# Splitting a router's dispatch into single-instruction steps, and moving its sums, in a two-layer transformer kernel

## The chip, the cores and the metric

The kernel runs on one core of one Trainium2 chip. The metric is the device time of one execution in microseconds (us), less is better. A core has five engines that run their own instruction streams: TensorE (PE, matrix products), VectorE (DVE), ScalarE (ACT), GpSimd (POOL), and SyncE (SP), which here only issues DMAs. PE writes its results to the memory PSUM, whose parts are called banks; the other engines read them from there. Everything else on the chip lies in SBUF.

## The reference

Two transformer layers on x of 4 batch elements x 1024 tokens x 256 features, all in float32. Layer 0 is attention with 16 heads, normalised queries and keys and rotary positions, followed by a gated feed-forward. Layer 1 is causal attention with 8 heads, followed by a mixture of experts. After each of the four parts the input is added and a layer norm is taken. The change concerns the mixture of experts, whose core is:

```python
xn = _rmsnorm(x_flat, norm_weight, EPS)
probs = softmax(xn @ router_weight.T + router_bias)
gate_vals, expert_idx = top_k(probs, 2)
pos = sum(cumsum(one_hot) * one_hot) - 1      # place in the expert's queue
keep = pos < CAP                              # CAP = 512
dispatch = zeros((16, CAP, 256)).at[expert, slot].add(xn[tok] * keep)
# expert 0: zeros; 1: copy of the row; 2, 3: constant vectors; 4 to 15: MLPs
w = gate_vals * keep
out = sum(expert_out[expert, slot] * w) / (sum(w) or 1)
x = layernorm(x + out)
```

Queues run over all tokens in order, so the positions of one batch element depend on the counts of those before it, and an expert's rows are complete only when the last element has been dispatched.

## The kernel before

**Stages.** For each element b there are four pieces of work: the first attention (`first_units(b)`, 64 units), the first feed-forward, the second attention (`second_units(b)`, 29 units) and the router with its dispatch. The program works on them in a weave: it goes through the units of one attention and sets pieces of other work behind each unit. Within this part nothing is rescheduled (`manual_schedule`): on every engine instructions stand in the order in which the code emits them. `later(n, fn)` puts a function off by n units; `tick()` at the start of a unit runs those due.

For elements 0 and 1, `weave` takes one step of `dispatch(b)` per unit of `first_units(b + 2)`, from unit `side_at` on. For element 2 and for the first half of element 3 ("3a") there is a hand-written table `plan`: `plan[u]` lists what follows unit u of `second_units(3)`. The second half of element 3 ("3b") follows after the last unit, then the twelve MLP experts one after another, about 29 us each, then the last layer norm.

**second_units.** A unit can hold: scores of one block of keys (`sc`, L964: four heads, each once with the keys and once with the maxima), values and denominators of the block before it (`av`, `dn`, L1001), and a maxima unit (`mx`, L914), whose four results DVE reduces (L924 on the diagonal, L928 elsewhere). Units 20 to 28 have no maxima. All these PE results and other "big" pieces share six PSUM banks in turn; a bank is free again when DVE or ACT has read it. ACT takes the exponential (L975), POOL zeroes the upper triangle on the diagonal (`affine_select`, L978), DVE takes reciprocals of the denominators (L1019), POOL multiplies with them (L1021). Behind the units stand the output projection (`ppa`, L572) with its residual addition and statistics on DVE (L539 to L542), the roots on POOL (L105), the normalisation on DVE (L109), the transposition of x for the router (`ptxn`, L622) and the logits (`pl`, L693).

**dispatch.** Its steps are: `choose(0)` and `choose(1)` (largest logits and their experts, L742 to L753), `queue` (counts, L758 to L761), `positions` (two matmuls into `pos`, L767 and L768, and their copy L769), `slots` (L774 to L785: the slot numbers `si`), `weights` (L789 to L805: weights `w`, the row's tail `meta`, the shares `we`), `stage` (L815, L818: two rows xn and their tails in `st`), `send` (two indirect DMAs of one row of 128 tokens to `disp_d`, issued by POOL, L824) and `base` (three multiply-adds on DVE that add the copy's and the constant vectors' shares to x, L836 and L840, then a store of x to `acc_d` on SP, L843). For elements 0 and 1 one step was `send` and `base` of one row of tokens. For elements 2 and 3 the `base` functions, "sums", were emitted behind the ordered part, so that the scheduler set them in between:

```python
        for step in steps3[10:] + more:
            step()
        ordered.close()
        for step in sums2 + sums3 + sums:
            step()
```

**Behind it.** `load_rows(0)` loads the first expert's rows in four parts (L1408, waiting for every send), `transpose_to` turns them (`ptd`, L98) and copies them to `dmT` (L99), `ph` (L1439) and `py` (L1455) are the expert's two products, and an indirect DMA adds its results to `acc_d` (L1459), for expert 0 only after the stores of all sums. The pools for `dm`, `dmT` and others take over the memory of the pools before them, x among it.

Of the kernel before, what the change touches and what calls it, by code (L numbers as in the profile page):

```python
# [19 lines left out]
P = 128  # L20
# [15 lines left out]
def postln_layers_kernel(ctx: ExitStack, tc: tile.TileContext, a: dict, out: bass.AP):  # L36
# [53 lines left out]
    spacer = const.tile([P, 1], F32, name="spacer")  # L90


    def transpose_to(dst, src, pool, name):

        n = dst.shape[1]
        pt = pool.tile([P, 512], F32, tag="m", name=name)
        for i in range(n):
            nc.tensor.transpose(pt[:, i * P : (i + 1) * P], src(i), ident)  # L98
        nc.any.tensor_copy(dst, pt[:, : n * P].rearrange("p (n q) -> p n q", n=n))  # L99
# [11 lines left out]
    with ExitStack() as main:  # L111
# [598 lines left out]
        def dispatch(b, big, part=None):  # L710
# [20 lines left out]
            def choose(k):  # L731
# [3 lines left out]
                if k == 0:  # L735
# [3 lines left out]
                    for key in ("g", "ei", "pk", "keep", "w", "step"):  # L739
                        v[key] = act.tile([P, 2, n], F32, tag=f"v_{key}", bufs=1, name=f"{key}_{name}")  # L740
# [21 lines left out]

            def positions():

                flat = v["both"].rearrange("p t e -> p (t e)")
                pos = bank(f"pos_{name}", big)[:, : n * E]
                nc.tensor.matmul(pos, before, flat, start=True, stop=False)  # L767
                nc.tensor.matmul(pos, ones, v["cum"].rearrange("p t e -> p (t e)"), start=False, stop=True)  # L768
                nc.vector.tensor_copy(flat, pos)  # L769

            def slots():
                pk, keep, w, ei, step = [v[key] for key in ("pk", "keep", "w", "ei", "step")]
# [3 lines left out]
                none = none_f[:, :, rows]  # L776
                nc.vector.tensor_scalar(keep, pk, float(CAP), None, ALU.is_lt)
                nc.vector.tensor_tensor(w, w, keep, ALU.mult)
                nc.vector.tensor_scalar(step, ei, -float(EM), None, ALU.is_ge)
                nc.vector.tensor_tensor(keep, keep, step, ALU.mult)  # L780
                nc.vector.scalar_tensor_tensor(pk, ei, float(CAP), pk, ALU.mult, ALU.add)
                nc.vector.scalar_tensor_tensor(pk, pk, float(NSLOT), none, ALU.add, ALU.subtract)
# [4 lines left out]
            def weights():  # L787
                gs, gz, w = small("gs"), small("gz"), v["w"]
# [5 lines left out]
                v["meta"] = meta = act.tile([P, n, 4], F32, tag="v_meta", bufs=1, name=f"meta_{name}")  # L794
                nc.vector.tensor_copy(meta[:, :, 0], v["ei"][:, 0])
                nc.vector.tensor_tensor(meta[:, :, 1], w[:, 0], w[:, 1], ALU.subtract)
                nc.vector.tensor_copy(meta[:, :, 2], w[:, 1])
                nc.vector.tensor_copy(meta[:, :, 3].bitcast(I32), tok_i[:, rows])
                v["we"] = we = act.tile([P, n, 3], F32, tag="v_we", bufs=3, name=f"we_{name}")
                wo = v["oh", 1][:, :, 1:4]  # L800
                for k, t in enumerate((we, wo)):
                    nc.vector.tensor_tensor(
                        t, v["oh", k][:, :, 1:4], w[:, k].unsqueeze(2).to_broadcast([P, n, 3]), ALU.mult
# [9 lines left out]
            def stage(i):  # L813
                v["st", i] = st = late_tile(b, [P, 2, ROW], F32, "xn", 12, f"row_{name}_{i}")
                nc.vector.tensor_copy(st[:, :, C:ROW], v["meta"][:, 2 * i : 2 * i + 2, :])  # L815
                for t in (2 * i, 2 * i + 1):
                    r, u = st[:, t % 2, :], first + t
                    nc.vector.scalar_tensor_tensor(r[:, 0:C], xs[b, u], rrs[b][:, u : u + 1], nw, ALU.mult, ALU.mult)  # L818
# [15 lines left out]
            def base(t):  # L834
                x, u = xs[b, first + t], first + t
                nc.vector.scalar_tensor_tensor(  # L836
                    x, v["st", t // 2][:, t % 2, 0:C], v["we"][:, t, 0:1], x, ALU.mult, ALU.add
                )
                for k in range(2):
                    nc.vector.scalar_tensor_tensor(  # L840
                        x, v["cv"][:, k], v["we"][:, t, 1 + k : 2 + k], x, ALU.mult, ALU.add
                    )
                based.append(nc.sync.dma_start(acc_rows[:, b * TB + u, :], x).ins)  # L843
                if b + 2 < B:
                    load_x(b + 2, u)

            def both_steps(t):
                send(t)
                base(t)

            out = [lambda: choose(0), lambda: choose(1), queue, positions, slots, weights]
            if b < B - 2:
                for i in range(n // 2):
                    out += [lambda i=i: stage(i), lambda i=i: both_steps(2 * i), lambda i=i: both_steps(2 * i + 1)]
                return out
            out += [lambda i=i: stage(i) for i in range(n // 2)] + [lambda t=t: send(t) for t in range(n)]
            return out, [lambda t=t: base(t) for t in range(n)]

        sent, based = [], []

# [437 lines left out]
        for b in (1, 2):  # L1298
# [16 lines left out]
                30,  # L1315
# [25 lines left out]
        steps2, sums2 = dispatch(2, True)  # L1341
        steps3, sums3 = dispatch(3, True, 0)
# [15 lines left out]
        for u, step in enumerate(steps2[:5]):  # L1358
            plan[12 + u].append(step)
        plan[17] += steps2[5:8]  # L1360
        plan[18] += steps2[8:10]
        for u, step in enumerate(steps2[10:]):
            plan[18 + u].append(step)
        for u, p in ((16, out3[0]), (17, out3[1]), (18, tu[0]), (19, lo[0]), (19, tu[1]), (20, lo[1])):
            plan[u].append(lambda p=p: p(True))
        for u, step in enumerate(steps3[:5]):
            plan[21 + u].append(step)
        plan[26] += steps3[5:8]
        for u in range(2):
            plan[27 + u].append(steps3[8 + u])  # L1370
# [17 lines left out]
        more, sums = dispatch(3, True, 1)  # L1388
        for step in steps3[10:] + more:
# [188 lines left out]
```

## Time and profile before

| | |
|---|---|
| median of 3 runs | 2486.8 us (2482.63 to 2492.3) |
| profiled execution, its own time | 2493.76 us |
| its span, first to last instruction | 2492.0 us |
| mean granted TensorE clock | 0.949 |
| second_units(3), first maxima to last values | 1887 to 2060 us |
| element 3's last projection to the first expert | 2062 to 2107.6 us |
| twelve experts | 2107.6 to 2458 us |

All durations below are of the one profiled execution. A line of the timeline has the start and the time of a group in us, the engine, the line of the code, the operation, what it writes and reads, how many instructions it has, and in brackets how long the engine stood idle ahead of it and who released it. A line of the windows has start and end, length, busy time of the engine with its instructions, granted clock, share of the DMA engines and GB/s. DVE operations of a dozen to a hundred elements take 0.16 to 0.29 us, one of 256 elements 0.4 to 0.5.

### The profile page before, as it was taken

The page shows a single profiled execution, that of the slowest core. Times are in us where ns is not written, and L with a number is a line of the kernel's source. Part 1 is how long each engine was busy: PE and PEld are TensorE (multiplying, and loading weights), DVE is VectorE, ACT ScalarE, POOL GpSimd, SP SyncE. Part 2 cuts the span into 40 slices and gives each one's busy share as a digit, 9 for nine tenths or more (in the row PEclk, how much of TensorE's full clock was granted, in tenths as well). Part 3 has the DMA queues.
Part 4 walks back from the last instruction along what each step waited for, and adds up shares of the span by engine and source line. Part 5 has one row for each costly group of instructions (what it writes and reads, how often), then busy time and mean ns, then how long its engine had stood idle before and what let it go on. Part 6 is the DMA issues. An engine that isn't in the chain of part 4 may idle for free.

```text
span 2492.0 us, 36155 instructions
## 1 busy us (share of the span) xinstructions
PE 2331.3 (94%) x14004; PEld 1156.8 (46%) x14004; DVE 1384.9 (56%) x3227; ACT 1020.2 (41%) x2037; POOL 743.9 (30%) x1101
## 2 busy tenths in 40 slices
PE   7999998999999999999999999999999974999994
PEld 4433333444444443444444434445556432666662
DVE  6666664766656556686574767806645674111113
ACT  2465554554552445545433464462232231111112
POOL 5234536125204132363051420301112154212223
PEclk9999998999998999999899999998999686999997
DMA  3124212000000000011000000102000012444434
GB/s 96 56 95 143 70 44 70 1 27 1 1 27 1 1 1 1 23 46 33 32 1 1 1 1 1 62 7 99 1 1 1 1 52 69 102 107 114 105 88 146
DMA packets 78124, 107.77 MB, mean 43 GB/s; under 512 B 8832, under 2 KB 67200, under 8 KB 76288
## 3 DMA queue, kind: packets, MB, share of 16 engines
q1 hardware_dynamic: 48592, 73.34, 9.0%
q0 software_dynamic: 9984, 14.82, 3.1%
q10 hardware_dynamic: 19376, 17.30, 2.3%
q8 instruction: 110, 1.80, 0.3%
q14 instruction: 62, 0.51, 0.1%
HBM read 66.54 MB, written 38.90 MB: 42 GB/s over the span
## 4 chain that ended last, share of the span: by engine, by line
PE 86%; DVE 7%; DMA 3%; POOL 2%; issue 1%; ACT 1%; SPq 0%; DVEq 0%; ACTq 0%; POOLq 0%
PE sc L474 19%; PE av L492 10%; PE ph L1439 7%; PE gu L638 7%; PE py L1455 7%; PE sc L964 5%; PE mx L914 4%; PE mx L450 4%; PE p L883 4%; PE dn L654 4%; PE av L1001 3%; PE dn L1001 2%; PE ppa L572 2%; DVE masked L924 2%; PE qk L303 2%; PE pt L441 1%
## 5 line engine op out<-in xcount | busy, mean ns | idle before, releaser
L453 DVE TENSOR_REDUCE part<-mx 128x1 f32<-128x512 f32 x1024 | 655.6, 683 | 338.0 <-PE mx L450 331.7
L483 ACT ACTIVATE pe<-sc 128x512 f32<-128x512 f32 x1024 | 554.2, 596 | 401.5 <-PE mx L450 349.2
L450 PE MATMUL mx<-kT,qT 32*128 32x512 f32 x2048 | 631.4, 646 | 2.1 <-DVE part L453 1.9
L474 PE MATMUL sc<-qT,kT 32*128 32x512 f32 x2048 | 606.4, 639 | 0.0
L474 PEld LDWEIGHTS sc<-qT,kT 32*128 32x128 f32 x2048 | 176.4, 183 | 220.3 <-issue 178.4
L492 PE MATMUL av<-pe,va 128*32 128x512 f32 x2048 | 273.9, 607 | 0.0
L975 ACT ACTIVATE pe<-sc 128x512 f32<-128x512 f32 (+3 forms) x384 | 157.2, 496 | 216.8 <-PE sc L964 216.5
L450 PEld LDWEIGHTS mx<-kT,qT 32*128 32x128 f32 x2048 | 188.2, 185 | 40.0 <-DVE part L453 18.6
L924 DVE CUSTOM_DVE_ANT_0 masked<-mx,mask_w 128x128 bf16<-128x128 f32 (+3 forms) x256 | 125.2, 489 | 122.0 <-PE mx L914 89.8
L1439 PE MATMUL ph<-dmT,f 128*128 128x512 f32 x384 | 170.5, 602 | 4.3 <-DVE dmT L99 3.5
L1447 ACT ACTIVATE hTm<-ph,b 128x512 f32<-128x512 f32 x96 | 60.8, 684 | 261.5 <-PE ph L1439 261.5
L1455 PE MATMUL py<-f,hTm 128*128 128x256 f32 x768 | 167.7, 379 | 0.0
L978 POOL TENSOR_SCALAR_AFFINE_SELECT pe<-pe 128x256 f32<-128x256 f32 x128 | 54.4, 434 | 370.7 <-ACT pe L975 369.2
L1459 POOL DMA_INDIRECT acc_d<-yo,dm x48 | 74.7, 1556 | 285.3 <-DVE yo L1457 233.9
L1455 PEld LDWEIGHTS py<-f,hTm 128*128 128x128 f32 x768 | 145.9, 190 | 25.0 <-issue 5.7
L914 PE MATMUL mx<-kT,qT 32*128 32x512 f32 (+3 forms) x768 | 142.4, 593 | 3.8 <-DVE x L539 3.2
L368 POOL TENSOR_TENSOR ss<-ss,neg_half 128x16 f32<-128x16 f32 x48 | 139.2, 2908 | 0.5
L964 PE MATMUL sc<-qT,kT 32*128 32x512 f32 (+3 forms) x768 | 133.6, 591 | 4.0 <-DVE part L924 2.5
L1456 DVE TENSOR_TENSOR yo<-py,b 128x256 f32<-128x256 f32 x48 | 20.4, 425 | 208.1 <-PE py L1455 208.1
L492 PEld LDWEIGHTS av<-pe,va 128*32 128x32 f32 x2048 | 40.5, 108 | 194.1 <-issue 188.7
L1439 PEld LDWEIGHTS ph<-dmT,f 128*128 128x128 f32 x384 | 72.9, 192 | 95.0 <-issue 86.9
L638 PE MATMUL gu<-xTf,wg 128*128 128x256 f32 x384 | 107.2, 401 | 0.3 <-ACT pe L975 0.3
(346 smaller groups left out, 2976.9 us busy)
## 6 DMA issues: line engine op xcount, KB each, us to landing
f<-in_fc SPq DMA_DIRECT2D x14, 1024.0 KB, 4.9
f<-in_fc ACTq DMA_DIRECT2D x10, 1024.0 KB, 5.9
disp_d<-empty ACTq DMA_DIRECT2D x12, 520.0 KB, 3.4
xink<-in_xT SPq DMA_DIRECT2D x24, 256.0 KB, 3.2
qk_d<-xs SPq DMA_DIRECT2D x6, 1024.0 KB, 3.9
xr<-qk_d SPq DMA_DIRECT2D x6, 1024.0 KB, 6.1
dm<-disp_d SPq DMA_DIRECT2D x11, 520.0 KB, 3.6
x<-in_x SPq DMA_DIRECT2D x32, 128.0 KB, 2.9
```

The costliest lines, as they stand in the source:

```text
L450: nc.tensor.matmul(sc, self.qT[r, t * P : (t + 1) * P], self.kT[r, u * 512 : (u + 1) * 512], start=True, stop=True)
L453: return lambda: nc.vector.tensor_reduce(self.part[:, t, u, h : h + 1], sc, AX.X, ALU.max, negate=True)
L474: nc.tensor.matmul(sc, self.m.kT[r, kt * P : (kt + 1) * P], self.m.qT[r, qb * 512 : (qb + 1) * 512], start=True, stop=True)
L483: nc.scalar.activation(self.pes[i, h // 2][:, h % 2, :], sc, AF.Exp)
L492: nc.tensor.matmul(self.av[32 * h : 32 * h + 32, :], va0[:, kt, 4 * self.g + h, :], self.pes[i, h // 2][:, h % 2, :], start=kt == 0, stop= ...
L638: nc.tensor.matmul(ps[:, i * 256 : (i + 1) * 256], w[:, c, f * P : (f + 1) * P], xT[j][:, c, :], start=c == 0, stop=c == 1,)
L914: nc.tensor.matmul(scs[h][:, :n], qT[r, t * P : (t + 1) * P], kT[r, u * 512 : u * 512 + n], start=True, stop=True,)
L924: nc.vector.tensor_tensor_reduce(masked[:, :n], scs[h][:, :n], mask_w[:, 512 - n :], -1.0, -NEG, ALU.add, ALU.min, part)
L964: nc.tensor.matmul(scs[h][:, off:], ones_h[r, :] if w else kT[r, kt * P : (kt + 1) * P], (self.m.nmT if w else qT)[r, q], start=w == 0, st ...
L975: nc.scalar.activation(pe[:, j, off:], scs[2 * hp + j][:, off:], AF.Exp)
L1439: nc.tensor.matmul(ph[:, i * CAP : (i + 1) * CAP], f1[:, c, (f + i) * P : (f + i + 1) * P], dmT[:, c, :], start=c == 0, stop=c == 1,)
L1455: nc.tensor.matmul(py[:, :C], hT[:, f, c * P : (c + 1) * P], f2[:, f, :], start=f == 0, stop=f == FF1 // P - 1)
```

## The change

The steps of the dispatch are cut smaller and set anew. What needs no positions (`prepare`, `row`) is a step of its own ahead of what does; `positions` is split from its copy `places`; `shares` is split from `weights`; a row's tail (`ends`) is split from the row. For elements 0 and 1 every multiply-add of a sum is a step of its own, and the steps begin at unit 26. In the plan element 2's sums follow units 20 to 27, three multiply-adds each, and the turn and logits of element 3's x come one unit later. Element 3's sums come behind its last send and behind the load of the first expert's rows, whose tile is now in another pool; all of it is in the ordered part. Both copies of expert 0's turned rows go to ACT, and an extra Gelu instruction (`spacer2`) loads ACT's table ahead of them.

```diff
@@ dispatch
+            def prepare():
+                ei, none = v["ei"], none_f[:, :, rows]
+                nc.vector.tensor_scalar(v["step"], ei, -float(EM), None, ALU.is_ge)
+                nc.vector.tensor_scalar(v["at"], ei, float(CAP), float(NSLOT), ALU.mult, ALU.add)
+                nc.vector.tensor_tensor(v["at"], v["at"], none, ALU.subtract)
...
+                nc.vector.tensor_copy(meta[:, :, 0], ei[:, 0])
+                nc.vector.tensor_copy(meta[:, :, 3].bitcast(I32), tok_i[:, rows])
             def positions():
...
-                nc.vector.tensor_copy(flat, pos)
+            def places():
+                nc.vector.tensor_copy(v["both"].rearrange("p t e -> p (t e)"), v["pos"])
             def slots():
...
-                nc.vector.tensor_scalar(step, ei, -float(EM), None, ALU.is_ge)
-                nc.vector.tensor_tensor(keep, keep, step, ALU.mult)
-                nc.vector.scalar_tensor_tensor(pk, ei, float(CAP), pk, ALU.mult, ALU.add)
-                nc.vector.scalar_tensor_tensor(pk, pk, float(NSLOT), none, ALU.add, ALU.subtract)
+                nc.vector.tensor_tensor(keep, keep, v["step"], ALU.mult)
+                nc.vector.tensor_tensor(pk, pk, v["at"], ALU.add)
...
+            def row(t):
+                u = first + t
+                nc.vector.scalar_tensor_tensor(
+                    staged(t // 2)[:, t % 2, 0:C], xs[b, u], rrs[b][:, u : u + 1], nw, ALU.mult, ALU.mult
+                )
+            def ends(i):
+                nc.vector.tensor_copy(staged(i)[:, :, C:ROW], v["meta"][:, 2 * i : 2 * i + 2, :])
...
+            def base(t, k):
...
+                vec = v["cv"][:, k - 1] if k else v["st", t // 2][:, t % 2, 0:C]
+                nc.vector.scalar_tensor_tensor(x, vec, v["we"][:, t, k : k + 1], x, ALU.mult, ALU.add)
+                if k == 2:
+                    based.append(nc.sync.dma_start(acc_rows[:, b * TB + u, :], x).ins)
...
+            if b < B - 2:
+                out += [at_once(queue, prepare), at_once(positions, places), slots, at_once(weights, shares)]
+                for t in range(n):
+                    out.append(rows_[t] if t % 2 else at_once(ends_[t // 2], rows_[t]))
+                    out += [at_once(sends[t], bases[t][0]), *bases[t][1:]]
+                return out
+            steps = out + [queue, positions, prepare, places, slots, weights]
+            return steps, rows_, ends_, sends, [shares] + [fn for fns in bases for fn in fns]
@@ weave of elements 0 and 1
                 dispatch(b - 1, False),
-                30,
+                26,
@@ plan of second_units(3)
+        plan[12] += steps2[:1]
+        plan[13] += steps2[1:2]
+        plan[14] += steps2[2:3] + steps2[4:5]
+        plan[15] += steps2[3:4] + steps2[5:6] + rows2[:1]
+        plan[16] += steps2[6:7] + rows2[1:3]
+        plan[17] += steps2[7:8] + ends2 + sums2[:1] + rows2[3:4]
+        plan[18] += rows2[4:6]
+        plan[19] += rows2[6:8]
+        for u, step in enumerate(sends2):
             plan[18 + u].append(step)
-        for u, p in ((16, out3[0]), (17, out3[1]), (18, tu[0]), (19, lo[0]), (19, tu[1]), (20, lo[1])):
+        for u, step in enumerate(sums2[1:]):
+            plan[20 + u // 3].append(step)
+        for u, p in ((16, out3[0]), (17, out3[1]), (19, tu[0]), (20, lo[0]), (20, tu[1]), (21, lo[1])):
             plan[u].append(lambda p=p: p(True))
...
+        plan[22] += steps3[:1]
+        plan[23] += steps3[1:2]
+        plan[24] += steps3[2:3] + steps3[4:5]
+        plan[25] += steps3[3:4] + steps3[5:6] + rows3[:1]
+        plan[26] += steps3[6:7] + rows3[1:3]
+        plan[27] += steps3[7:8] + ends3 + sums3[:1] + rows3[3:]
+        plan[28] += sends3[:1]
@@ behind the units
-        more, sums = dispatch(3, True, 1)
-        for step in steps3[10:] + more:
+        steps, rows, ends_, sends, sums = dispatch(3, True, 1)
+        for step in sends3[1:] + steps[:5] + rows[:1] + steps[5:] + ends_ + rows[1:] + sends:
             step()
+        nc.scalar.activation(spacer2, ones[:, 0:1], AF.Gelu)
+        dm0 = tail.tile([P, ECH, ROW], F32, name="dm0")
+        load_rows(0, dm0)
+        for step in sums3[1:] + sums:
+            step()
         ordered.close()
-        for step in sums2 + sums3 + sums:
-            step()
@@ experts
+                nc.any.tensor_copy if e else nc.scalar.copy,
```

The pairs of a row (`stage`, `both_steps`) are gone. In `weights` the two copies to `meta` that `prepare` now has, and the three operations of `shares`, are cut out; their text is the same.

## The prediction

> **What bounds the kernel now.** I read the page first (busy shares, the 40 slices), then the chain of waits, then PE's waits from 1885 to 2062 us, and last the timeline of DVE, POOL and SP there and up to 2110 us.
>
> ```profile
> span 2492.0 us, 36155 instructions
> PE 2331.3 (94%) x14004; PEld 1156.8 (46%) x14004; DVE 1384.9 (56%) x3227; ACT 1020.2 (41%) x2037; POOL 743.9 (30%) x1101
> ...
> PE   7999998999999999999999999999999974999994
> ...
> PEclk9999998999998999999899999998999686999997
> ```
> PE is the bound nearly everywhere. Slices 33 and 34 (1994 to 2118 us) are the exception, at 7 and 4 tenths: the second half of element 3's second attention and the dispatch behind it. The waits of PE in that attention, as total, times, longest:
>
> ```profile
> PE ptxn L622 <- DVE x L109: 10.4, 2, 5.4
> PE ptm L944 <- DVE nm L937: 3.3, 1, 3.3
> PE mx L914 <- DVE x L539: 2.7, 2, 2.2
> PE av L1001 <- POOL pe L978: 1.6, 1, 1.6
> ```
> All but the ptm (at 1900, before any edit) lie between 1998 and 2059. The same places in PE's timeline, then two stretches of it for DVE alone:
>
> ```profile
> 2007.67 1.12 PE L914 MATMUL mx<-kT,qT 32*128 32x512 f32 x2 [2.16 <-DVE x L539]
> 2013.77 1.12 PE L622 MATMUL ptxn<-ident,x 128*128 128x128 f32 x4 [4.98 <-DVE x L109]
> 2025.55 1.13 PE L622 MATMUL ptxn<-ident,x 128*128 128x128 f32 x4 [5.42 <-DVE x L109]
> 2031.48 2.09 PE L964 MATMUL sc<-qT,kT 32*128 32x512 f32 x8
> ```
> ```profile
> 2006.00:2026.60 20.60, 19.90 (x60) 0.77 0.22 77
> 2026.60:2060.00 33.40, 20.38 (x69) 0.84 0.20 73
> ```
> DVE is full for 20.6 us, while PE waits for normalised rows queued in it, and then has 13 us free: element 2's 24 sums (L836, L840) stand in the full part. The end of the dispatch is a pure chain:
>
> ```profile
> 2088.23 0.96 POOL L824 DMA_INDIRECT disp_d<-row_3b,si_3b  x1 [9.71 <-DVE row_3b L818]
> ...
> 2092.34 2.46 POOL L824 DMA_INDIRECT disp_d<-row_3b,si_3b  x1 [0.20 <-issue]
> ...
> 2098.90 0.96 POOL L824 DMA_INDIRECT disp_d<-row_3b,si_3b  x1 [0.19 <-issue]
> 2101.90 2.22 SPq L1408 DMA_DIRECT2D dm<-disp_d  x5
> ...
> 2106.93 0.59 ACT L99 COPY dmT<-ptd 128x512 f32<-128x512 f32 x1 [25.55 <-DMA dm<-disp_d]
> ...
> 2107.57 16.46 PE L1439 MATMUL ph<-dmT,f 128*128 128x512 f32 x32 [0.58 <-ACT dmT L99]
> ```
> Positions, eight sends, their landing, the load of the first rows, transposes, copies; PE does nothing else meanwhile. From 2107.57 twelve experts run at 29.0 us each; the change leaves them alone.
>
> **What the Trainium skill says.** The Trainium skill, "TensorE: Matmul & The Clock Gate", Part 1: PE runs at half clock after an idle window of about 3.4 us and needs as long a busy one to recover. The trace agrees: the sc group above takes 2.09 us behind the 5.42 us wait and 1.14 us at 2039. The Trainium skill, "DMA: Bandwidth & Descriptors", Anatomy of one DMA: a wait is held by the issuing sequencer, not by the DMA engines, so what is queued behind a waiting DMA isn't issued. That decides the order on SP below; the page's fixed cost of about 2 us stands beside 2.43 us for a send and 1.7 us (median) for a store of a row of sums here. The Trainium skill, "ScalarE: Activation LUTs", What ACT_TABLE_LOAD costs: about 1.28 us for the load; here 1.28 us at 2107.54.
>
> **The change part by part**
>
> *Elements 0 and 1* (dispatch inside first_units(2) and (3)): 18 steps from unit 30 become 38 from unit 26, the last in unit 63, so none spills. The operations stay, with one small one more (five in prepare, one in slots, for three in slots and two in weights), 0.17 us. PE's waits of this kind are small there: 1.6 us for a maximum at 1060 to 1100, under 1 us in 1300 to 1640. Element 2's and 3's x loads come up to 16 units later, but the row concerned is first needed a dozen units into the next weave. Bounds -2 and +1; I take a gain of 0.2.
>
> *Element 2's router and rows, units 14 to 19.* Five prepare operations (0.6 us) go ahead of the maxima of unit 15, behind which DVE had 1.94 us free: nothing. Row 0 (0.43) fits there too. In unit 16 slots loses two operations (0.4), but rows 1 and 2 (0.85) stand ahead of the residual additions whose PSUM bank PE wants: the 0.54 us wait grows to about 1.1. In unit 17 weights, four tails, shares and row 3 take 2.2 us ahead of the next additions, where DVE now has 3.8 us of them and some sums: the 2.16 us wait falls to about 0.4. The turn of element 3's x stands one unit later and no sum is ahead of its normalise: DVE reaches it at about 2009.2, PE at about 2011. The 4.98 goes. The second, at 5.42, goes too: DVE's 33 us of work from 1992 lose 24 sums at 0.39 us from start to start (9.4 us) and reach the second pair at about 2016, before PE. Late next are PSUM banks: two scores units wait for reductions (0.8) and for masked ones, four at 0.85 us (1.3), and the mask turn for nm (0.5). Left over: 1.1 + 0.4 + 0.8 + 1.3 + 0.5 = 4.1 of 0.54 + 2.16 + 4.98 + 5.42 = 13.1. **Gain 9.0.**
>
> *The clock.* From 2013.8 to 2039.4 the groups at half clock cost 6.5 us over the same groups when warm (the sc and nmT pairs 2.8, av and dn 1.25, pl 0.8, turns 1.0, a narrow sc 0.7). Gaps of 4 us are gone, but narrow matmuls and gaps of 1 us stay. Between nothing and 6.5; I take **2.0**, as 1930 to 1951 shows half clock with no such gap.
>
> *Element 2's sums in units 20 to 27*: 1.2 to 1.3 us per unit; the 12 sums of 3a (5 us) leave. DVE's list from the mask's copy to unit 27's last row adds up to 26.4 us, PE's work to 24.9, with at most 1 us of wait at pos_3a. Cost nothing, but with no cover left. Only one send pair of 3a is left, behind the last affine_selects: those no longer wait for POOL at 2058 (gain 1.2), but that pair ends about 0.4 us after the first reciprocal of the last quotient. **Gain 0.8.**
>
> *The end.* Six sends of 3a instead of four lie between the roots and the first 3b send; POOL is through at 2081, 7 us early. Prepare and row 0 (1.05 us) stand where DVE waited 0.57 us for pos: 0.48 more. After it slots is two operations shorter (0.45), two copies of weights and three operations of shares are gone (0.5), and so is the pair of rows ahead of the first send (0.85), for one tail more (0.08): first send at about 2087.0 instead of 2088.23, **gain 1.2**. The slow send of 2.46 us (others 0.96) coincides with four stores of sums on SP, and these now come later: between 0 and 1.8, taken **0.9**. The load waits for 9 semaphores instead of 19, at 28 ns (the median of SP's event semaphores): **0.4**.
>
> The added wait: in the built program the ACT copy of the first dmT waits for all eight stores of element 3's sums, as its pool takes over memory of theirs, and these now stand on SP *behind* the first load. From the first load's issue S: four loads to S + 1.3, stores at 0.35 us each; the last four use semaphores of the loads and wait for them to land, the eighth until about S + 4.3; it lands 1.7 us later, S + 6.0; copy 0.6: first matmul at S + 6.7. Before: 2107.57 - 2101.90 = 5.67. **Loss 1.0**, bounds 0 and 4. Both copies on ACT: the second is done 0.6 us after the first, before its matmul 0.86 us on. The Gelu load (1.28) leaves a place where ACT idled 4.95 us until 2113.77: nothing. The sums, 24 at 0.39 us, are done before 2099, and expert 0's scatter at 2129 is far off. Expert 1's rows are issued at S + 6, needed at 2137.
>
> Sum: 0.2 + 9.0 + 2.0 + 0.8 + 1.2 + 0.9 + 0.4 - 1.0 = **13.5 us**. The profiled execution took 2493.8 (span 2492.0 and 1.8 around it) and would take 2480.3; the median of the runs shown, 2486.8, lies 7.0 below it, and the same gain gives **2473.3**.
>
> **Rivals**
>
> *A, the forecast*: 2473.3, own range 2470 to 2477. Chance 0.52.
>
> *B, the wait moves to units 21 to 27.* DVE there has no slack. Were the sums 0.16 us longer (L840's mean is 594 ns in elements 0 and 1, 472 in element 2), 24 x 0.16 = 3.8 us would end at pos_3a and the last reciprocals, and 2 of the clock's gain would go: 2479.1. For it: 26.4 against 24.9. Against: 0.39 from start to start in the full stretch. Chance 0.19.
>
> *C, the clock comes back whole* and half of the remaining 4.1 goes: 4.5 + 2.0 more: 2466.8. For it: 1992 to 2009 at clock 1.00. Against: 1930 to 1951. Chance 0.24.
>
> *D, slower*: the eight stores behind the first load run one after another, each waiting for its forerunner's landing: 8 x (0.35 + 1.7) = 16.4 from S + 4.3, the first matmul at S + 21.3, 15.6 later than before instead of 1.0: 2487.9. Place: SP, lanes shared with the loads. It decides once the stores cost 14.5 us, 1.8 each. Against: four stores took 3.17 us in all at 2091. Chance 0.05.
>
> That the change doesn't do what it says: the sums might have stayed where they were; the built order shows them moved, so it gets nothing of its own.
>
> **How the numbers follow.** The likeliest is A. The range, 2466 to 2483, takes in C, most of B, and three us of scatter (runs shown lie from 2482.6 to 2492.3). A measurement tells 0.5%, 12.4 us, from no change: 2474.4 is the edge. Of A some 0.62 lies below, all of C, nothing of B and D: 0.52 x 0.62 + 0.24 = 0.56. Slower by over 0.5% (2499.2) is D and more: 0.03. Same 0.41.
>
> **What would show it.** ptxn's waits for the normalise under 1 us in all; sc of the second group near 2018 instead of 2031; the second attention over by 2047 in the profile; first 3b send 4.2 us after pos instead of 5.4; ACT's first dmT copy released by a store of sums, not by the load. Wrong, if PE waits over 3 us at pos_3a (B), if the stores hold ph beyond S + 9 (D), or if the slow clock spreads beyond its old stretches.

## The result, and the profile after

| | before | after |
|---|---|---|
| median of 6 runs | 2489.92 us (2482.63 to 2492.3) | 2473.45 us (2470.76 to 2475.98) |
| ratio, 95% interval | | 0.9937 [0.9923, 0.9952] |
| profiled execution | 2493.76 us | 2474.32 us |
| mean granted clock | 0.949 | 0.953 |

The forecast for the median was 2473.3 us. The page of the kernel after, as far as it answers to what was shown of before:

```profile
span 2472.6 us, 36148 instructions
PE 2321.8 (94%) x14004; PEld 1153.8 (47%) x14004; DVE 1380.7 (56%) x3231; ACT 1020.3 (41%) x2039; POOL 737.6 (30%) x1101
...
PE   7999998999999999999999999999999994999994
...
PEclk8999999999998999999899999999999686999997
```

Slice 33 is full now, slice 34 still stands at 4, and PE is busy 9.5 us less with the same 14004 matmuls. That last figure is the first surprise: where only waits go, busy time stays.

Where the time went is read by pairing PE's matmuls of the two traces and taking the start after minus the start before. The 19.4 us between the spans of the two profiled executions divide so (places in us of before; a dispatch is taken from the first router step that either kernel has to the last sum):

```
stretch                                                PE's gain
1010-1220 and 1480-1665  (elements 0, 1 dispatched)    3.9 + 3.6 = 7.5
1985-2058                (second attention, el. 3)     7.1
2058-2150                (end, first expert)          -0.4
all the rest             (unchanged code)              5.2
```

The forecast had 0.2, 11.8 and 1.5 for the first three. The rest lies where both kernels run the same code, under other half-clock windows; 2.3 us of it are there before the first dispatch begins. PE's timeline of the kernel after in the second attention, all groups behind a wait of over 0.55 us from 1985 to the first projection:

```profile
1987.99 0.92 PE L944 MATMUL mx<-kT,qT 32*128 32x384 f32 x6 [1.11 <-DVE x L540]
...
2005.38 0.61 PE L974 MATMUL ptm<-ident_h,nm 128*128 128x128 bf16 x4 [1.08 <-DVE nm L967]
...
2025.26 1.70 PE L994 MATMUL sc<-qT,kT 32*128 32x512 f32 x2 [1.48 <-ACT pe L1005]
...
2044.07 5.78 PE L573 MATMUL ppa<-w1o,oT 128*128 128x256 f32 x14 [3.06 <-POOL oT L1051]
```

The 4.98 and 5.42 us at the normalise are gone, as forecast. The last two lines are new or longer: 1.48 us at the scores was not there, and the first projection waits 3.06 instead of 1.72 us, which before had so:

```profile
2062.04 4.21 PE L572 MATMUL ppa<-w1o,oT 128*128 128x256 f32 x9 [1.72 <-POOL oT L1021]
```

The chain of waits at the end of the dispatch:

```profile
2078.39 2.52 DMA disp_d<-row_3b,si_3b
2081.06 0.32 SPq L885
...
2082.91 0.37 SPq L856
...
2085.80 0.40 SPq L856
2086.29 1.78 DMA acc_d<-x
2088.17 0.59 ACT dmT L100
```

The last send lands, the load is issued, then the stores of element 3's sums, and the copy of the first `dmT` waits for the last of these: 7.75 us from the load's issue to the first `ph`, 5.67 before.

### The profile page after: what moved, and what is told of

It is laid out like the page before. It is cut to its first block, busy times and chain, and to the rows that moved or that the text cites. A ratio compares the mean times of both kernels' runs of the same rounds, so it can differ in the third digit from the quotient of the medians.

```text
span 2472.6 us, 36148 instructions
## 1 busy us (share of the span) xinstructions
PE 2321.8 (94%) x14004; PEld 1153.8 (47%) x14004; DVE 1380.7 (56%) x3231; ACT 1020.3 (41%) x2039; POOL 737.6 (30%) x1101
## 4 chain that ended last, share of the span: by engine, by line
PE 86%; DVE 8%; DMA 2%; issue 1%; ACT 1%; POOL 1%; SPq 0%; DVEq 0%; POOLq 0%; ACTq 0%
PE sc L475 20%; PE av L493 10%; PE ph L1470 7%; PE py L1486 7%; PE gu L639 7%; PE sc L994 5%; PE mx L944 4%; PE p L913 4%; PE mx L451 4%; PE dn L655 4%; PE av L1031 3%; PE dn L1031 2%; DVE masked L954 2%; PE ppa L573 2%; PE qk L304 2%; PE pt L442 1%
## 5 line engine op out<-in xcount | busy, mean ns | idle before, releaser
L451 PE MATMUL mx<-kT,qT 32*128 32x512 f32 x2048 | 623.4, 647 | 0.2 <-DVE part L454 0.2
L954 DVE CUSTOM_DVE_ANT_0 masked<-mx,mask_w 128x128 bf16<-128x128 f32 (+3 forms) x256 | 125.5, 490 | 114.6 <-PE mx L944 81.6
L840 POOL DMA_INDIRECT disp_d<-row,si x48 | 48.4, 1007 | 222.3 <-DVE row L829 216.1
```

Source lines behind the costliest of these rows:

```text
L451: nc.tensor.matmul(sc, self.qT[r, t * P : (t + 1) * P], self.kT[r, u * 512 : (u + 1) * 512], start=True, stop=True)
L954: nc.vector.tensor_tensor_reduce(masked[:, :n], scs[h][:, :n], mask_w[:, 512 - n :], -1.0, -NEG, ALU.add, ALU.min, part)
```

## Why the weaves gained: a stall that is no idle time

Element 1's dispatch, PE, one group of eight 32-row matmuls (four of the scores `sc`, four of the maxima `mx`) between its neighbours. Before:

```profile
1568.11 1.07 PE L492 MATMUL av<-pe,va 128*32 128x512 f32 x8
1569.11 0.69 PE L474 MATMUL sc<-qT,kT 32*128 32x512 f32 x1
1569.11 0.69 PE L450 MATMUL mx<-kT,qT 32*128 32x512 f32 x1
1569.12 1.11 PE L474 MATMUL sc<-qT,kT 32*128 32x512 f32 x2
1569.65 0.59 PE L450 MATMUL mx<-kT,qT 32*128 32x512 f32 x1
1569.65 0.59 PE L474 MATMUL sc<-qT,kT 32*128 32x512 f32 x1
1570.05 1.12 PE L450 MATMUL mx<-kT,qT 32*128 32x512 f32 x2
```

After, the same kind of group:

```profile
1561.58 0.69 PE L475 MATMUL sc<-qT,kT 32*128 32x512 f32 x1
1561.59 0.69 PE L451 MATMUL mx<-kT,qT 32*128 32x512 f32 x1
1561.60 0.69 PE L475 MATMUL sc<-qT,kT 32*128 32x512 f32 x1
1561.61 0.69 PE L451 MATMUL mx<-kT,qT 32*128 32x512 f32 x1
1562.12 0.59 PE L475 MATMUL sc<-qT,kT 32*128 32x512 f32 x1
```

Four matmuls start within 0.03 us and run side by side, each on 32 of the array's rows; a group of eight takes two such fours, 1.06 us. The Trainium skill, "TensorEngine Tiling (Array Packing)", Tiling Modes, says that tiles operate independently and can run matmuls in parallel; the trace agrees. It follows, and the trace of before shows, that one late member makes a four into two halves: in before the third start is a pair of scores one behind the other, the maxima follow at 1570.05, and the next group starts at 1571.10, 1.99 us from the first instead of 1.07. No bracket stands in any line, since something always ran. What was late is seen on DVE, which frees the PSUM banks of the maxima. Before:

```profile
1567.09 0.48 DVE L836 SCALAR_TENSOR_TENSOR x<-row,we,x 128x256 f32<-128x256 f32 x1
1567.61 1.00 DVE L840 SCALAR_TENSOR_TENSOR x<-cv,we,x 128x256 f32<-128x256 f32 x2
...
1569.32 2.58 DVE L453 TENSOR_REDUCE part<-mx 128x1 f32<-128x512 f32 x4
```

Three multiply-adds of one sum, 1.5 us, and then four reductions in one row, two of them late. After, one multiply-add, and the reductions come in pairs:

```profile
1559.57 0.48 DVE L854 SCALAR_TENSOR_TENSOR x<-row,we,x 128x256 f32<-128x256 f32 x1
...
1560.84 1.28 DVE L454 TENSOR_REDUCE part<-mx 128x1 f32<-128x512 f32 x2
```

Counting all groups of four scores and four maxima at 1036 to 1110 and 1520 to 1610, where before has most of its dispatch, and what those that ran over 1.36 us took beyond 1.06:

```
                 long groups   their excess   PE's gain, both dispatches whole
before              10            8.0 us            -
grouped26            7            5.5              -3.8
sums_whole           3            2.0               3.8
rows_whole           2            1.5               6.6
weaves_alone         1            0.5               7.5
after                1            0.5               7.5
```

The kernels named are those of the experiments below. Three things make the changed kernel faster in these places: the long groups, 7.5 us; waits that do show (`mx` behind L453, 1.9 us before and 0.2 after), 1.7; and a half-clock window of 3.4 us at 1089 that is gone, worth some 1.7 (one long group lies in it in part, so that about 0.5 is counted twice). Against them stands a price ahead of these places. The dispatch begins earlier, and PE meets the router's steps there: its lead falls by 3.1 us between 1018 and 1036, with waits of 0.77 us behind `hT` (L650) and 0.96 us behind the copy of `pos` (L781), and by 1.4 us between 1500 and 1520. What is left is 7.5 us, and 7.5 again in the other traces with this dispatch (8.1 in behind_act); 1 to 2 us of the account are not assigned.

## The experiments

Each ran in five rounds beside the kernel before. All times in us:

```
kernel                  median    ratio, 95% interval        at clock 0.954
before                                                       2484
after                   2473.45   0.9937 [0.9923, 0.9952]    2472
weaves_alone            2477.27   0.9960 [0.9947, 0.9972]    2476
grouped26               2478.19   0.9962 [0.9950, 0.9974]    2479
sums_whole              2471.17   0.9943 [0.9922, 0.9965]    2476
rows_whole              2472.77   0.9948 [0.9928, 0.9968]    2473
sums2_late              2470.50   0.9925 [0.9912, 0.9937]    2472
early_turns             2479.72   0.9961 [0.9946, 0.9976]    2475
late_sums_early_turns   2475.41   0.9947 [0.9932, 0.9962]    2475
sums2_split             2471.10   0.9931 [0.9917, 0.9945]    2474
stores_first            2473.65   0.9946 [0.9934, 0.9958]    2473
split_act_stores        2462.70   0.9910 [0.9891, 0.9928]    2470
later_turns_act         2467.27   0.9922 [0.9906, 0.9938]    2469
behind_act              2458.07   0.9883 [0.9863, 0.9902]    2466
```

Most intervals overlap, and much of the spread is PE's clock. The last column is an estimate that takes it out. Over 123 timed runs of these kernels and of before the time falls by 1.8 us for each 0.001 of mean granted clock, and runs of one kernel scatter by 1.2 us about a line of that slope; the column is read off these lines at a clock of 0.954, each to within about 1 us. What a kernel gains by keeping the clock up is taken out too.

### The weaves: weaves_alone, grouped26, sums_whole, rows_whole

**weaves_alone** is the kernel before with the changed dispatch for elements 0 and 1 only:

```diff
-                dispatch(b - 1, False),
-                30,
+                dispatch_single(b - 1, False),
+                26,
```

> The kernel before with one part of the change alone: elements 0 and 1 are dispatched in 38 single steps from unit 26 of their weaves instead of 18 grouped steps from unit 30; plan, end and transposes stay as before. Theory (the two traces: PE is some 8 us ahead by 1720 us): about 8 us less than before, ratio 0.9968, and PE ahead by 6 to 10 us at 1720. Rival (the forecast's 0.2 us; the lead in one profiled execution is scatter of the clock): ratio 0.9999, within 0.001 of 1, and PE ahead by less than 3 us at 1720. If both hold half, 4 us.

Measured: 0.9960, 10.0 us of the 2487.88 us of the kernel before, timed beside it (8 at equal clock). The theory held, and the forecast's 0.2 us fell. In its second attention all the old waits are still there (2.16, 4.98, 5.43), so the gain is that of the weaves. Its trace is 18.8 us ahead soon after 1720, which goes beyond what was expected: 7.5 of it lie in the two dispatches, 8.6 were there before the first of them began, and the rest too lies in unchanged code, under other half-clock windows.

**grouped26** begins in unit 26 but groups as before, **sums_whole** groups only the sums, **rows_whole** only the rows:

```diff
-                for t in range(n):
-                    out.append(rows_[t] if t % 2 else at_once(ends_[t // 2], rows_[t]))
-                    out += [at_once(sends[t], bases[t][0]), *bases[t][1:]]
+                for i in range(n // 2):
+                    out.append(at_once(ends_[i], rows_[2 * i], rows_[2 * i + 1]))
+                    out += [at_once(sends[t], *bases[t]) for t in (2 * i, 2 * i + 1)]
```

> The changed kernel with the steps of elements 0 and 1 grouped as before (two rows at once, a send and its three sums at once), but begun in unit 26 as in the change. Theory that DVE's long bursts are what cost time (three sums in a row ahead of a reduction that PE waits for): the weaves' gain of 8 us is lost, ratio to before 0.997. Rival that the earlier begin is what counts (rows, sums and x loads done by unit 44, out of the way of the later units): the gain stays, 0.9937 as the changed kernel. Rival that the weaves bring nothing: 0.9937 too, and then the kernel with the weaves alone shows no gain either.

> The changed kernel with, in elements 0 and 1, each send and its three sums as one step again; rows stay single, begin in unit 26. Theory that a burst of 1.5 us of sums ahead of a reduction breaks PE's fours of 32-row matmuls without showing as idle time: of the 4.5 us by which groups of eight such matmuls around the dispatch run longer in the kernel with both grouped, most (3 or more) returns, and the time is 3 to 6 us above the changed kernel, ratio 0.9955. Rival that the pair of rows is the long burst: little returns, 0.994.

> The changed kernel with, in elements 0 and 1, the two rows of a pair and their tail as one step again; sums stay single, begin in unit 26. Theory (the sums' bursts of 1.5 us count, those of rows, 1.1 us, less): the groups of eight lose under 2 us, ratio 0.9940. Rival (rows count as much): 0.9955.

Measured: with both grouped the dispatches no longer gain 7.5 us but lose 3.8 (there a wait of 2.59 us behind `hT` does show, at 1107.88, with half clock around it), and the ratio rises to 0.9962: the earlier begin by itself brings nothing, the cut into single instructions does. With one of the two grouped, half of the gain or more stays (3.8 and 6.6 us). The timed ratios, 0.9943 and 0.9948, cannot be told from the changed kernel's, and of the long groups' excess only 1.5 us returns with the sums, not 3. But in the traces grouped sums cost 3.7 us and grouped rows 0.9, and at equal clock 4 and under 1. So the order that the theory named shows. What it did not name is that both together cost 7 us at equal clock and 11 in the trace, far more than the sum of the two. Why, was not tried further.

### The second attention: sums2_late, early_turns, late_sums_early_turns, sums2_split

The forecast put the gain down to element 2's 24 sums leaving DVE's queue ahead of the normalises. But the change also turned element 3's x one unit later. Two places for the sums, two for the turns:

```diff
 sums2_late: the sums written behind the plan, the scheduler puts them back into units 17 to 20
-        for u, step in enumerate(sums2[1:]):
-            plan[20 + u // 3].append(step)
...
+        for step in sums2[1:]:
+            step()
 early_turns
-        for u, p in ((16, out3[0]), (17, out3[1]), (19, tu[0]), (20, lo[0]), (20, tu[1]), (21, lo[1])):
+        for u, p in ((16, out3[0]), (17, out3[1]), (18, tu[0]), (19, lo[0]), (19, tu[1]), (20, lo[1])):
```

> The changed kernel with element 2's 24 sums written after the second attention's plan instead of in it, so that they stand where they stood before the change, behind the rows of units 17 to 20, ahead of element 3's normalises. Theory of the forecast: the two waits for the normalises come back (10.4 us before, 0.2 in the changed kernel), some 9 us of wait at 2000 to 2026; less what the sums take in units 24 to 27 (the 1.5 us wait for ACT at 2025 goes, 1 to 3 us): 6 to 9 us slower than the changed kernel, ratio to before 0.9965. Rival (the normalises were late for other reasons: three steps at once in unit 17, turns one unit earlier): ptxn's waits under 2 us, ratio 0.994.

> The changed kernel with the turns and logits of element 3's first half back in the units where they stood before (18, 19, 19, 20 instead of 19, 20, 20, 21); element 2's sums stay in units 20 to 27. Theory that either of the two moves is enough to let DVE reach the normalises in time: as the changed kernel, within 2 us, ratio 0.9937, ptxn's waits under 2 us. Rival that the turns' later place is what brought the gain of the second attention: ptxn's waits of 5 us or more come back and the kernel is 4 to 6 us slower, ratio 0.996.

> The kernel with element 2's sums behind the rows as before the change (sums2_late), and the turns too in their old units. Theory (either move suffices, neither doesn't): the two waits of 5 us come back, 5 to 8 us slower than sums2_late, ratio to before 0.9950; the gain that is left is that of the weaves, 0.996, and some of the end. Rival (the gain of the second attention comes from something else, as the single rows or the twelve sums that left units 26 to 28): ratio as sums2_late, 0.9925, with the waits below 6 us.

PE's waits over 0.55 us at maxima, normalises, mask turns and scores between 1985 and the last values, and PE's gain on before from 1985 to 2150:

```
kernel                  sums in   turns in   waits                          sum    gain
before                  17-19     18, 19     2.16 + 4.98 + 5.42            12.6     -
late_sums_early_turns   17-20     18, 19     1.12 + 0.87 + 5.62 + 4.06     11.7     3.2
early_turns             20-27     18, 19     1.12 + 2.38 + 4.06 + 1.65      9.2     2.9
sums2_late              17-20     19, 20     1.12 + 0.86 + 2.61 + 0.94      5.5     9.8
after                   20-27     19, 20     1.11 + 1.08 + 1.48             3.7     6.7
```

The lines behind it, early_turns first:

```profile
2001.45 1.14 PE L623 MATMUL ptxn<-ident,x 128*128 128x128 f32 x4 [2.38 <-DVE x L110]
...
2013.27 1.13 PE L623 MATMUL ptxn<-ident,x 128*128 128x128 f32 x4 [4.06 <-DVE x L110]
```

then sums2_late, where no normalise is waited for in the attention, though 18 of the 24 sums still stand ahead of the second one on DVE (all 24 before, 18 in late_sums_early_turns, none in early_turns):

```profile
1997.45 0.70 PE L944 MATMUL mx<-kT,qT 32*128 32x512 f32 x3 [0.86 <-DVE x L540]
...
2001.61 1.39 PE L994 MATMUL sc<-qT,kT 32*128 32x256 f32 x3 [2.61 <-DVE part L958]
```

The theory that either move suffices fell. With the turns early, 0.9961 and 0.9947 are no better than the weaves alone (0.9960); with the turns late, 0.9925 and 0.9937. It is the place of the turns that brought the gain: PE has a whole unit of its own matmuls to do before it comes to the rows that DVE still has to normalise. At equal clock the turns are worth 2 and 3 us, with the sums late and early on DVE. Moving the sums out brought nothing (0.9925 [0.9912, 0.9937] with them ahead). The gains in the table tell no more than that: grouped26, sums_whole and rows_whole run the code of after from 1985 on, and gain 6.3, 8.7 and 10.4 us there. So 6.7 and 9.8 cannot be told apart, while gains of 3 lie clearly below both.

**Why not**, one sees at 2025 in the kernel after. ACT's and DVE's timelines:

```profile
2024.52 0.20 ACT L754 ACTIVATE w_3a<-w_3a 128x4 f32<-128x4 f32 x1 [4.82 <-DVE w_3a L752]
2024.63 2.04 ACT L1005 ACTIVATE pe<-sc 128x512 f32<-128x512 f32 x4
```
```profile
2021.75 0.38 DVE L854 SCALAR_TENSOR_TENSOR x<-row,we,x 128x256 f32<-128x256 f32 x1
2022.16 1.08 DVE L854 SCALAR_TENSOR_TENSOR x<-cvs,we,x 128x256 f32<-128x256 f32 x2
...
2024.33 0.15 DVE L752 TENSOR_TENSOR w_3a<-g_3a 128x4 f32<-128x4 f32 x1
```

The sums of units 20 to 23 put off element 3's second choice on DVE; its exponential `w_3a` stands in ACT's queue ahead of the attention's exponentials, so ACT idles 4.82 us, and PE, which needs the scores' banks back, waits 1.48 us, and its clock is half from 2025.2 to 2032. The unit's work from its first scores to `pos_3a` takes 9.09 us there (2022.65 to 2031.74) and took 3.30 in before (2042.57 to 2045.87): 5.8 us more. The wait alone does not make all of it. Two other traces have the same wait of 1.48 us at a full clock, rows_whole and stores_first, and their unit takes 6.2 us. So the wait costs 2.9 us, and the half clock, where it comes, 2.9 more.

**sums2_split** writes twelve sums behind the plan and twelve in units 20 to 25:

```diff
-        for u, step in enumerate(sums2[1:]):
-            plan[20 + u // 3].append(step)
+        for u, step in enumerate(sums2[13:]):
+            plan[20 + u // 2].append(step)
```

> The changed kernel with the first twelve of element 2's sums behind the rows (units 17 to 20) and the other twelve in units 20 to 25, two a unit. Theory (both places are short of DVE time for 24 sums: in the early one PE waits 5.3 us for a normalise and a maximum, in the late one 4.6 us for the exponentials and quotients behind them): twelve fit in each, both sets of waits fall below 2 us, 3 to 5 us faster than the better of the two, ratio 0.991. Rival (the waits come from elsewhere than the sums): as sums2_late or the changed kernel, 0.9925 to 0.9937.

Measured 0.9931, a miss: the late waits went, the early 2.60 at the scores stayed, as the first sums, ahead of the reductions L958 on DVE, are in that place in both. It stands where sums2_late stands.

### The end: stores_first, split_act_stores, later_turns_act

```diff
 stores_first
+        for step in sums3[1:] + sums:
+            step()
         nc.scalar.activation(spacer2, ones[:, 0:1], AF.Gelu)
         dm0 = tail.tile([P, ECH, ROW], F32, name="dm0")
         load_rows(0, dm0)
-        for step in sums3[1:] + sums:
-            step()
 split_act_stores: sums2_split, and
-                    based.append(nc.sync.dma_start(acc_rows[:, b * TB + u, :], x).ins)
+                    based.append((nc.sync if part is None else nc.scalar).dma_start(acc_rows[:, b * TB + u, :], x).ins)
```

> The changed kernel with element 3's sums written ahead of the first load instead of behind it: DVE's order stays, SP issues the eight stores before the four loads. Theory (the copy of the first dmT waits for the last store, 2.1 us): from the load's issue to the first matmul of the experts 5.7 us instead of 7.75, the copy released by PE or the load: 2 us less, ratio 0.9929. Rival (the stores beside the sends make a send slow, as the 2.46 us one of before, and the load later): a send over 1.8 us, gain under 0.7, ratio 0.9935. Rival that the load's own landing sets it: 7.7 us again.

> The kernel with the sums split, and the eight stores of element 3's sums issued by ACT instead of SP, each as soon as its sum is there, while SP issues the first load behind the sends. Theory (the copy of the first dmT waited for stores that stood behind the load on SP): from the start of the last send to the first matmul of the experts 8.2 us instead of 10.4 in the changed kernel and 9.6 with the stores first, 2.2 us faster than the split alone, ratio 0.990. Rival (stores in flight beside the sends slow a send, as in before): a send above 1.8 us and the gain under 1 us.

From the start of the last send to the first `ph`, from the timelines:

```
                   last send   load issued   first ph   from the last send
before             2098.90     2101.90       2107.57      8.67
after              2078.39     2081.06       2088.81     10.42
stores_first       2063.06     2067.32       2072.69      9.63
split_act_stores   2070.01     2072.77       2077.93      7.92
```

That the copy waited for the stores is shown: with them ahead, the load's issue to `ph` is 5.37 us, not 7.75. But no expectation of stores_first named what took 1.6 of the 2.4 us back: no send was slow (the longest 1.14); SP stood at the last store for the last sum, which DVE ends at 2066.7, and the load behind it could not be issued (2067.32, 4.26 us behind the last send instead of 2.67). The Trainium skill, "DMA: Bandwidth & Descriptors", Anatomy of one DMA, has the wait on the issuing sequencer; here it shows on both sides, stores behind a load and a load behind stores. The timed ratio of stores_first, 0.9946, is no better than the changed kernel's 0.9937. From ACT's queue neither waits for the other: the way from the last send to `ph` is 2.5 us shorter than in the changed kernel, and no send is slow. For split_act_stores it is 0.9910 against the split's 0.9931; their intervals overlap, so the timelines carry the verdict: 7.7 to 7.9 us in the three kernels with ACT's stores, 10.4 in all eight with the stores behind the load. One sees the two queues in split_act_stores:

```profile
2063.10 12.11 ACTq L856 DMA_DIRECT2D acc_d<-x  x8
...
2072.77 5.20 SPq L885 DMA_DIRECT2D dm<-disp_d  x6
```

**later_turns_act** is sums2_late with the turns yet a unit later, `(20, tu[0]), (21, lo[0]), (21, tu[1]), (22, lo[1])`, and the stores by ACT.

> Element 2's sums behind the rows as before the change, element 3's turns and logits in units 20, 21, 21, 22 (one unit later than in the change, two later than before), and element 3's stores issued by ACT. Theory (it is the place of the turns that decides whether DVE's queue shows on PE): the 2.7 and 2.6 us of wait at the normalise and the maximum of sums2_late fall below 1.5 together, unless the first choice of element 3 then comes late at pos_3a (under 1 us); with 2.2 us of the stores, 5 to 6 us faster than sums2_late, ratio 0.990. Rival (DVE's sums delay maxima too, whatever stands between): the maxima's wait of 2.6 stays, ratio 0.9915.

Measured 0.9922: a miss for the theory. The 2.60 at the scores stays and 1.36 us comes behind it (L954). One unit was enough to take the normalises off the path; the maxima are delayed by the sums themselves, as the rival said.

### A version that beats both: behind_act

```diff
@@ choose / prepare
-                    nc.scalar.activation(v["w"][:, 1], v["w"][:, 1], AF.Exp)
...
+                nc.scalar.activation(v["w"][:, 1], v["w"][:, 1], AF.Exp)
                 ei, none = v["ei"], none_f[:, :, rows]
@@ plan
-        for u, step in enumerate(sums2[1:]):
-            plan[20 + u // 3].append(step)
...
         plan[28] += sends3[:1]
+        for u, step in enumerate(sums2[1:]):
+            plan[20 + u // 4].append(step)
```

and the stores by ACT as above.

> The changed kernel with element 3's stores issued by ACT, element 2's sums four a unit in units 20 to 25, each behind the router step of its unit instead of ahead of it, none in 26 and 27, and the exponential of the second choice issued one step later (with the prepared values). Theory (with the turns in place the 24 sums cost PE time only where an ACT or POOL step stands behind a DVE step that they delay): the 1.48 us wait of the scores for ACT goes, that of the last quotient falls from 3.06 to 1.8, and the stores give 2.5 from the last send to the experts' first matmul: 5 us faster than the changed kernel, ratio 0.9915. Rival (DVE's load as such decides, 24 sums in six units are too many): another wait of 1.5 us or more between the turns and the end of the attention, and only the 2.5 us of the stores, 0.9927.

Measured 2458.07 us, 0.9883 [0.9863, 0.9902], below the changed kernel's interval and better than the 0.9915 expected; the interval of split_act_stores overlaps it. PE's waits over 0.55 us between 1990 and the first projection:

```profile
1991.93 0.61 PE L974 MATMUL ptm<-ident_h,nm 128*128 128x128 bf16 x4 [0.94 <-DVE nm L967]
...
2012.91 0.43 PE L777 MATMUL pos_3a<-oh_3a,before 128*128 128x64 f32 x2 [0.77 <-DVE oh_3a L758]
...
2015.65 2.47 PE L1031 MATMUL av<-pe,va 128*32 128x512 f32 x8 [0.58 <-issue]
...
2026.72 3.29 PE L573 MATMUL ppa<-w1o,oT 128*128 128x256 f32 x14 [1.77 <-POOL oT L1051]
```

The 1.48 at the scores is gone, 3.06 has become 1.77, and the last send to `ph` is 7.90 us. From 1985 to 2150 it gains 15.3 us on before, the changed kernel 6.7. So 24 sums do fit there without such a wait. The three edits were not tried one by one. Much of the timed lead over the changed kernel is clock: its six runs have mean clocks of 0.955 to 0.962, those of the changed kernel 0.952 to 0.955, and at equal clock the lead is 6 to 7 us, near the 5 expected. In its profiled execution some 10 us between 1900 and 1985, in unchanged code, are clock (last section).

## Why the prediction came out right

The number was right, 2473.3 against 2473.45, but two of its terms were wrong in opposite directions, and that they cancelled was luck. In the traces the changed code gains 7.5 + 7.1 - 0.4 = 14.2 us where the forecast had 13.5, in other places than it said.

- **"I take a gain of 0.2"** for elements 0 and 1 is the largest mis-sized term: 10.0 us timed alone, 7.5 in the trace. The step that failed is the sentence before it, that PE's waits of this kind are small there. They are, 1.6 us; but waits were read from idle time, and 7.5 us of stall stood inside groups of eight that ran long.
- **"Gain 9.0"**, the clock's **2.0** and **"Gain 0.8"** were 11.8 together; the trace gives 7.1 up to 2058, and 5.1 to 10.1 in three other traces with the same code. The waits named did go. The mechanism was half right: the same paragraph has both "the turn of element 3's x stands one unit later" and the 24 sums that DVE loses, and makes the sum with the latter. The runs show that the turn alone does it.
- **"Cost nothing, but with no cover left"** for the sums in units 20 to 27 is the step that took the difference: 5.8 us in the unit before `pos_3a` (2.9 where the clock stays full) and 1.3 at the last quotient. This is near what rival B described, in its place and of its size (3.8), though its sign, a wait over 3 us at `pos_3a`, did not come: what came late was not the positions but an exponential in ACT's queue, which the list of DVE's and PE's work did not contain. The clock's own term came out by chance: half clock lasts 20.5 us in before and 13.7 after from 1985 to the last values, worth 3.4, and 6.8 to 20.5 us in the three other traces.
- **The end, 1.5.** First send 4.40 us after `pos` instead of 5.45: 1.05 (forecast 1.2). First to last send 9.35 instead of 10.67, the slow one gone: 1.3 (0.9). Last send to load 2.67 instead of 3.00: 0.3 (0.4). The wait for the stores 2.1 (1.0; bounds 0 and 4): the cause was right, the last store was issued at S + 4.7 and landed at S + 7.0, against S + 4.3 and S + 6.0. With the 1.3 at the projection, nothing of the 1.5 is left.
- **The base.** 13.5 us were to come off 2493.8 and off 2486.8. The profiled pair lies 19.4 apart, the medians 16.5, the ratio gives 15.7 us of 2489.9; the median of before over six runs is 3.1 above that of the three shown. A forecast 2 to 6 us short of the change met a base 3 us low.
- **The signs.** The normalises' waits under 1 us, the release of the copy by a store and the sooner first send came true. The scores of the second group at 2008.5, and the attention over by 2044, are earlier than named, but 12 us of that lead were there at 1985 already.

## What to carry to other kernels

Where an engine runs small pieces side by side, time their groups against their own best case: a late member shows as a longer group and not as idle time. Ahead of an instruction that such a group waits for, cut the long steps of the engine in front into single instructions; and before a stall is put down to too much work ahead of it, ask what it costs to have the waiting side come a unit later. An instruction of one engine that waits for a late step of another holds all that stands behind it on its own queue: list those (here an exponential of four columns, eight stores) before calling a place free.

## What the hardware showed that was not expected

- A group of eight 32-row matmuls took 1.99 us instead of 1.07 without a gap on PE.
- The clock takes its own course. Between 1885 and 1980 us (places of before), in code that is the same, half clock lasted 44.4 us in before and after, 23.9 in stores_first and 10.2 in behind_act. The seven runs of stores_first lie from 2458.98 to 2476.68 us with mean clocks from 0.962 to 0.952. The prediction reads half clock from an idle window of about 3.4 us ahead of it. Some of the windows fit (3.35 us of wait end at 1902.89 in before, and half clock begins at 1904.3); that from 1931.6 has no wait of PE over 0.3 us in the 8 us ahead of it. What sets these is not shown. So single traces were compared stretch by stretch only, and the kernels by their medians.
- The same 1.48 us of wait went with half clock in three traces (after, grouped26, sums_whole) and not in two (rows_whole, stores_first). In after it doubled the matmuls from 2025.2 to 2032: the `av` group there took 1.94 us instead of 1.06. The unit took 9.1, 9.1 and 8.8 us in the three, 6.2 in the two.
